# Softplus of both layers by a cubic in two factors, and dt's bias as a row of a matrix product

## The chip, the cores and the metric

The kernel runs on one core of one Trainium2 chip. The metric is the device time of one execution in microseconds. A core has TensorE (PE: matrix products, into the eight banks of PSUM), VectorE (DVE), ScalarE (ACT), GpSimd (POOL) and SyncE (SP, which issues most of the DMAs). Each engine runs its own instructions in program order and waits at semaphores for the others.

## The reference

One image of 64 x 64 pixels with 96 channels goes through two layers. Each layer is a token mixer (a selective scan over the 4096 pixels, in several directions) and then an MLP 96 -> 384 -> 96 in an emulated 8-bit float. Both mixers compute, from the convolved and activated u (192 channels), a step length dt for every pixel and channel, and dt is what the change is about:

```python
x_dbl = u @ x_proj_w
dt = x_dbl[..., :DT_RANK]                                # 6 columns
B_mat, C_mat = ...                                       # 16 columns each
dt = jax.nn.softplus(dt @ dt_proj_w + dt_proj_b)
```

Then layer 0 forms `decay = exp(cumsum(dt * A))` and sums of `dt * B * u` weighted by it. Layer 1 runs the recurrence `h = exp(dt * A) * h + dt * u * B; y = sum(h * C)`, over 192 channels x 16 states, along rows and columns, forwards and backwards. For x of either sign, softplus(x) = max(x, 0) + log(1 + exp(-|x|)).

## The kernel before, in words

**The softplus.** ScalarE forms |t + bias| and from it z = sigmoid(-|t + bias| - ln 2); log(1 + exp(-|x|)) is z times a polynomial of degree four in z squared (`LOG1P`). VectorE forms the positive part and adds.

**Layer 0** (to about 104 us of the profile). `norm_in0` normalises the image and projects it. The decays of layer 0 fall to nothing so fast that only the first 160 steps at either end of each direction count (`scan_ends`): `x_proj(d)` makes the rows of four directions (L732, L733, copied by ScalarE at L734), `dt_proj(j)` makes t for three units of 128 x 320 (L739, L743) and gives ScalarE four operations each (L749 Abs, L750 Relu, L751 Sigmoid, L752 Square), and `log1p(j)` calls `polynomial` (L993, three times L995, L996, L997: six VectorE operations). The products of `x_proj` and `dt_proj` share a pool of two PSUM banks, which are taken in turn: four x_proj and three dt_proj in the order xe0, xe1, de0, xe2, xe3, de1, de2. The main convolution's taps (`conv0`, L644 and L645, its SiLU at L634) are put between by `others(n)`. All of it is kept in program order on every engine; on VectorE the casts of both MLPs' weights (L2496, L2500), which wait for their DMAs, come ahead of `scan_ends`. After `log1p` VectorE goes on with L792, the running sums of dt (L795) and their products (L807); ScalarE then loads a table and takes L816 and L828.

**The middle** (about 104 to 303 us). `middle` collects the rest of layer 0 and the beginning of layer 1 in an `Order`: every operation is added with its engine, an estimated cost in us, what it reads and writes and which buffers it takes. `Order.run` is a list scheduler. It plays the plan through with these costs, one operation at a time; among the operations that can start earliest it takes the one with the highest rank, which is the longest path to the end by the costs, plus the group's `LEAD`. The result is the program order of each engine. So costs and leads decide the order, and nothing else in the program. The groups are `mix0` (layer 0's gating and output, four pairs of chunks of 512 pixels), `compose1` (layer 1's convolution weights), `mlp0` (L1497 up, L1524 down, L1540 back, L1471 to L1477 `norm`, L1528 the bias), `conv_unit` (layer 1's convolution: products L1584 and L1586, combined by VectorE at L1611 to L1616, sigmoid L1619, u at L1620) and `project`. The projections wait for the last image rows (POOL, L1551), the sigmoids of `conv_unit` for the last square root of a norm.

`project(c, m, last)` runs four times: for (0,0), (0,1), (4,0) and (4,1), each on two chunks of 128 channels and half of the narrow 64. It makes x_dbl's rows (L1650, L1653) in two banks; ScalarE copies them to the buffer xd (L1656); `step_products` (L1695) and `step_products_n` (L1699) make t for three units of 128 x 512, in three banks. The weights lie twice in `w_dt1`, at partitions 0 to 5 and 96 to 101 (`RANKS`), filled by two DMAs (L1287) in `open1`. `softplus(i)` is the unit's work:

```python
o.add("ACT", 0.68, lambda: keep(act(vz(), at[t], AF.Abs, bias=bias)), ...)                 # L1714
o.add("DVE", 0.73, lambda: keep(dve.tensor_scalar(d(), at[t], bias, 0.0, ALU.add, ALU.max)), ...)   # L1715
o.add("ACT", 0.7, ... AF.Sigmoid ...)                                                      # L1716
o.add("ACT", 0.6, ... AF.Square ...)                                                       # L1717
o.add("DVE", 0.42, lambda: keep(dve.tensor_scalar(p(), vzz(), QC, QD, ALU.mult, ALU.add)), ...)     # L1718
```

and after that two more Squares on ScalarE (L1719, L1720) and three VectorE operations (L1721, L1722, L1723). `d` lies in the unit's dt buffer, `p` in its du buffer. Then dt times u is formed in the du buffer (L1727, L1730; POOL, in the last project VectorE), dt is copied by columns (L1736), and both are stored (L1767 to L1778). For the narrow units there is one dt and one du buffer (`ye`), for the wide ones two.

The last project also starts layer 1's scans: `spread4` products (L1807) repeat 32 rows of du and dt over 128 partitions, ScalarE copies them (L1821), VectorE multiplies (L1811) and makes the first two row scans (L1835).

**The scans** (L2014, from 302.7 us): 24 passes of 16 scans of 128 x 1024 on VectorE, with the decays on ScalarE (L1987), products and sums on POOL (L1966, L2019, L2042) and TensorE. Their order is written out by hand (`scans`). B's rows for the first passes are loaded on SP's queue behind the stores of the last project. At the end comes the last MLP.

Of the kernel before, what the change touches and what calls it, by code (L numbers as in the profile page):

```python
# [39 lines left out]
P = 128  # L40
# [21 lines left out]
RANKS = (slice(0, RANK), slice(96, 96 + RANK))  # L62
# [15 lines left out]
QA = LOG1P[3] / (4 * LOG1P[4])  # L78
QB = (LOG1P[2] / LOG1P[4] - 6 * QA**2) / 2
QC = LOG1P[1] - LOG1P[4] * (4 * QA**3 + 4 * QA * QB)  # L80
QD = LOG1P[0] - LOG1P[4] * (QA**2 + QB) ** 2

# [44 lines left out]
CARRIED = (0, 1, 2, 5, 7)  # L127
IN_DVE, OTHERS = (), (15, 9, 9)
# [10 lines left out]
LEAD = {"compose": -84.0}  # L139
LEAD |= {("mix", s): t for s, t in enumerate((1589.0, 1847.0, -1582.0, -1562.0))}  # L140
LEAD |= {("mlp", s): t for s, t in enumerate((1510.0, 80.0, 777.0, -2488.0))}
LEAD |= {("conv", 0, 0): 702.0, ("conv", 0, "n"): 2071.0, ("conv", 0, 1): -2872.0}
LEAD |= {("conv", 4, 0): -611.0, ("conv", 4, "n"): 13.0, ("conv", 4, 1): -2041.0}
LEAD |= {("project", 0, 0): -579.0, ("project", 0, 1): -3064.0, ("project", 4, 0): 470.0, ("project", 4, 1): -3512.0}
# [120 lines left out]
class Net:  # L265
    def __init__(self, ctx, tc, x, out):
# [23 lines left out]
        self.qa = self.column("qa", QA)  # L290
        self.qb = self.column("qb", QB)
# [399 lines left out]
    def scan_ends(self, ep, pm, ps, pad, ue, beside):  # L691
# [44 lines left out]
        def dt_proj(j):  # L736
# [13 lines left out]
            keep(nc.scalar.activation(dt[:, s, :], t, AF.Relu, bias=bias))  # L750
            keep(nc.scalar.activation(z[:, s, :], z[:, s, :], AF.Sigmoid, bias=self.nln2, scale=-1.0))  # L751
            keep(nc.scalar.activation(zz[:, s, :], z[:, s, :], AF.Square))  # L752

        def log1p(j):
            s = slice(2 * j, 2 * j + 2)
            self.polynomial(z[:, s, :], zz[:, s, :], dt[:, s, :], p[:, s, :], keep)
# [233 lines left out]
    def polynomial(self, z, zz, dt, p, keep):  # L990
# [6 lines left out]
        keep(nc.vector.tensor_tensor(dt, dt, p, ALU.add))  # L997

# [251 lines left out]
    def open1(self, w, kp, rp):  # L1250
# [35 lines left out]
        for r in RANKS:  # L1286
            nc.sync.dma_start(self.w_dt1[r], w["w_dt"])  # L1287
# [68 lines left out]
    def mix0(self, s):  # L1356
# [30 lines left out]
        for c in chunks:  # L1387
            o.add("PE", 0.95, mean(c), r=[("y0", c)], new={("m", c): "bank"})
        o.add("PE", 1.1, mean_n, r=both, w=[("m", c) for c in chunks])
        for c, r in zip(chunks, LANES):  # L1390
            o.add("DVE", 0.67, centre(c), r=[("m", c)], w=[("y0", c)])
            o.add("DVE", 0.67, centre_n(c, r), r=[("m", c)], w=[("y1", c)])
# [10 lines left out]
        for i, (key, y, r) in enumerate(squares):  # L1403
            o.add("PE", 0.95, variance(i, key), r=[key], **({"w": [("v", s)]} if i else {"new": {("v", s): "bank"}}))
# [1189 lines left out]
```

## Time and profile before

| what | value |
|---|---|
| median of 3 runs | 1218.54 us (1215.86 to 1219.69) |
| the profiled execution | 1217.9 us, span 1216.1 us |
| busy share of the span | PE 84%, DVE 93%, ACT 74%, POOL 69% |
| mean granted TensorE clock | 0.872 of full speed |
| first scan of L2014 starts | 302.72 us |
| last product of layer 1's convolution ends | 262.86 us |
| DMA | 183.10 MB, mean 151 GB/s |

A span is the time from the first to the last instruction of the profiled execution. In a list of groups each line has the source line, engine, operation, output <- inputs with their shapes and the count; then busy us, mean ns of one; then the engine's idle time before them and what ended it. In a timeline a line begins with the start and the duration in us, and the bracket tells the idle time before. PEclk is the share of TensorE's clock that was granted.

### The profile page before, as it was taken

What the parts mean: (1) busy time and instruction counts of PE and PEld (TensorE: products, weight loads), DVE (VectorE), ACT (ScalarE), POOL (GpSimd) and SP (SyncE); (2) the same over time, 40 slices, a digit from 0 to 9 for tenths busy, and PEclk for the clock granted to TensorE, in tenths of its full rate; (3) what the DMA queues carried; (4) which work ended last, traced back from release to release, by engine and by line L of the source; (5) the groups of instructions that cost most, each with busy time, mean ns of one, the idle gap of its engine ahead of it and who ended that gap; (6) DMA issues with size and microseconds to landing.
All of it is one profiled execution on the core that took longest, in us unless ns stands there. A gap on an engine that the chain in (4) does not pass through costs nothing.

```text
span 1216.1 us, 11204 instructions
## 1 busy us (share of the span) xinstructions
PE 1017.9 (84%) x3488; PEld 414.6 (34%) x3488; DVE 1129.2 (93%) x908; ACT 905.4 (74%) x1177; POOL 841.6 (69%) x510
## 2 busy tenths in 40 slices
PE   9998889985278877888888877898778898899886
PEld 5533333321023322222332322233224443344344
DVE  7895887688898999999999999999999999999978
ACT  5683654656578888887888878888888888898626
POOL 3002464352678888888798788988898887887756
PEclk9998999985589788798878788888789999888987
DMA  2262011376764583575734685545747767343301
GB/s 77 64 180 52 7 21 32 116 254 187 238 192 132 171 250 128 174 229 175 240 99 137 203 251 181 180 131 176 240 129 208 221 194 265 97 143 93 104 1 52
DMA packets 79128, 183.10 MB, mean 151 GB/s; under 512 B 21534, under 2 KB 34936, under 8 KB 77688
## 3 DMA queue, kind: packets, MB, share of 16 engines
q1 hardware_dynamic: 78376, 182.16, 48.2%
q8 instruction: 28, 0.46, 0.2%
q10 hardware_dynamic: 688, 0.19, 0.1%
q14 instruction: 36, 0.29, 0.1%
HBM read 159.73 MB, written 21.52 MB: 149 GB/s over the span
## 4 chain that ended last, share of the span: by engine, by line
DVE 37%; PE 19%; issue 8%; ACT 7%; DMA 3%; POOL 1%; SPq 0%; DVEq 0%; POOLq 0%; ACTq 0%
DVE xws L2014 12%; PE hs L2025 10%; DVE h1s L2014 10%; DVE h0s L2014 8%; PE hs L2029 4%; ACT da L1987 3%; DVE x2s L2014 3%; ACT xws L1972 2%; DVE x1s L2014 2%; DVE x0s L2014 2%; DMA kept<-xn 2%; DMA x2s<-bc 1%; PE acc L2053 1%; PE da L2343 1%; POOL hss L2019 1%
## 5 line engine op out<-in xcount | busy, mean ns | idle before, releaser
L2042 POOL TENSOR_TENSOR kept<-kept,kept 128x1024 f32<-128x1024 f32 x92 | 217.1, 2359 | 83.8 <-issue 45.0
L2019 POOL TENSOR_TENSOR hss<-h1s,xws 128x1024 f32<-128x1024 f32 x96 | 228.0, 2377 | 48.7 <-DVE xws L2014 47.1
L2025 PE MATMUL hs<-h0s,ident 128*128 128x512 f32 x360 | 224.8, 711 | 29.2 <-DVE h0s L2014 24.6
L1987 ACT ACTIVATE da<-dt1s,a 128x1024 f32<-128x1024 f32 x168 | 187.4, 1116 | 58.0 <-DVE xws L2014 49.0
L2014 DVE TENSOR_TENSOR_SCAN xws<-da,xws 128x1024 f32<-128x1024 f32 x96 | 221.5, 2307 | 7.3 <-ACT da L1987 7.2
L1987 ACT ACTIVATE da<-dt0s,a 128x1024 f32<-128x1024 f32 x166 | 185.2, 1115 | 27.2 <-DVE h0s L2014 10.0
L2029 PE MATMUL hs<-hss,ident 128*128 128x512 f32 x368 | 187.8, 602 | 8.1 <-POOL hss L2019 7.9
L2014 DVE TENSOR_TENSOR_SCAN h1s<-da,xws 128x1024 f32<-128x1024 f32 x69 | 156.0, 2261 | 0.0
L2053 PE MATMUL acc<-kept,fold 128*32 128x512 f32 x368 | 87.0, 683 | 71.8 <-POOL kept L2042 71.8
L2038 ACT COPY kept<-hs 128x512 f32<-128x512 f32 x184 | 107.7, 585 | 43.7 <-PE hs L2029 43.5
L2025 PEld LDWEIGHTS hs<-h0s,ident 128*128 128x128 f32 x360 | 72.4, 219 | 155.2 <-issue 82.4
L2029 PEld LDWEIGHTS hs<-hss,ident 128*128 128x128 f32 x368 | 70.3, 194 | 107.8 <-issue 79.4
L2025 PE MATMUL hs<-x1s,ident 128*128 128x512 f32 x128 | 75.7, 676 | 12.6 <-DVE x1s L2014 12.6
L2025 PE MATMUL hs<-x0s,ident 128*128 128x512 f32 x128 | 74.2, 664 | 13.5 <-DVE x0s L2014 13.5
L2025 PE MATMUL hs<-x2s,ident 128*128 128x512 f32 x120 | 72.9, 693 | 12.1 <-DVE x2s L2014 12.1
L1966 POOL TENSOR_TENSOR x1s<-x1s,dus 128x1024 f32<-128x1024 f32 x32 | 75.6, 2366 | 8.8 <-DMA x1s<-bc 8.8
L1966 POOL TENSOR_TENSOR x2s<-x2s,dus 128x1024 f32<-128x1024 f32 x32 | 75.7, 2366 | 1.3 <-DMA x2s<-bc 1.2
L2014 DVE TENSOR_TENSOR_SCAN x0s<-da,x0s 128x1024 f32<-128x1024 f32 x32 | 73.5, 2296 | 1.3 <-ACT da L1987 1.2
L2014 DVE TENSOR_TENSOR_SCAN x1s<-da,x1s 128x1024 f32<-128x1024 f32 x32 | 73.4, 2293 | 1.3 <-ACT da L1987 1.3
L2014 DVE TENSOR_TENSOR_SCAN x2s<-da,x2s 128x1024 f32<-128x1024 f32 x32 | 73.5, 2298 | 1.0 <-ACT da L1987 0.9
L1972 ACT COPY xws<-x1s 128x1024 f32<-128x1024 f32 x32 | 63.0, 1970 | 5.2 <-POOL hss L2019 5.2
L1966 POOL TENSOR_TENSOR x0s<-x0s,dus 128x1024 f32<-128x1024 f32 x28 | 66.3, 2367 | 0.0
(379 smaller groups left out, 1913.3 us busy)
## 6 DMA issues: line engine op xcount, KB each, us to landing
kept<-bc SPq DMA_DIRECT2D x92, 512.0 KB
x2s<-bc SPq DMA_DIRECT2D x32, 512.0 KB
x0s<-bc SPq DMA_DIRECT2D x28, 512.0 KB
x1s<-bc SPq DMA_DIRECT2D x28, 512.0 KB
dus<-du SPq DMA_DIRECT2D x20, 512.0 KB
dt1s<-dt SPq DMA_DIRECT2D x20, 512.0 KB
dt0s<-dt SPq DMA_DIRECT2D x20, 512.0 KB
kept<-xn SPq DMA_DIRECT2D x24, 384.0 KB
```

What stands on the lines that cost most here:

```text
L1966: keep(nc.gpsimd.tensor_tensor(x, x, du[:, part[j]], ALU.mult))
L1972: keep(copy(grid(xw)[:, w, :], cols(xs[i % 3])[:, w, :]))
L1987: keep(nc.scalar.activation(t, dts[o][:, part[j]], AF.Exp, scale=self.a6[:, g, k : k + 1]))
L2014: keep(nc.vector.tensor_tensor_scan(to, da, x, start, ALU.mult, ALU.add))
L2019: keep(nc.gpsimd.tensor_tensor(cols(hs)[:, w, :], grid(h1)[:, w, :], grid(xw)[:, w, :], ALU.add))
L2025: keep(nc.tensor.matmul(t, self.ident, x[:, chunk(m)], start=k == 0, stop=False))
L2029: keep(nc.tensor.matmul(sums[i, m], self.ident, hs[:, chunk(m)], start=False, stop=True))
L2038: keep(nc.scalar.copy(to, sums.pop((i, j * (SC // CH) + h))))
L2042: keep(nc.gpsimd.tensor_tensor(t, t, times_c_by(i, a), ALU.mult))
L2053: keep(nc.tensor.matmul(to, self.fold4, src, start=k == 0, stop=k == NK - 1))
L2343: keep(nc.tensor.matmul(o[:, j], y[r, 2 * k + j : CH : 4], w[r], start=first and j == 0, stop=end and j == 1))
```

## The change

In both layers log(1 + exp(-|x|)) becomes z times a cubic in z squared, written in two factors: z (zz + b)((s zz + a)^2 + c), with zz = z squared. The second factor's square is a ScalarE Square with a scale and a bias column; what remains are three VectorE operations.

- Layer 1, `softplus(i)`: ScalarE has Abs (without a bias), Sigmoid, Square, and a Square that writes into the du buffer. VectorE has three operations of three operands; the last takes the positive part of t from its PSUM bank and adds. L1715, L1718 and one Square are gone.
- dt's bias is a seventh row of `w_dt1`, filled by two more DMAs (a column of `vec` as one row of 256 numbers). The matching row of ones in xd comes from the copies of L1656, which become an Identity with the column `unit` as its bias; `unit` is made at the start by POOL.
- Layer 0: Relu moves from ScalarE to VectorE, emitted in `dt_proj`, ahead of all three `log1p`; the second factor's Square takes its place on ScalarE; `polynomial`'s six operations become two in `cubic` and an add.
- The middle's planner gets other costs for many operations and other leads. `norm` and `biased` get switches (`NORM0_ACT`, `BIAS0_POOL`) which are empty.

```diff
-RANKS = (slice(0, RANK), slice(96, 96 + RANK))
+RANKS = (slice(0, RANK + 1), slice(96, 96 + RANK + 1))
...
+CUBIC = (0.34226051, 1.83304455, -0.33816952, 3.07350780)
+QS = math.sqrt(CUBIC[0])
+QB = CUBIC[0] * CUBIC[3]
...
-LEAD = {"compose": -84.0}
-LEAD |= {("mix", s): t for s, t in enumerate((1589.0, 1847.0, -1582.0, -1562.0))}
-LEAD |= {("mlp", s): t for s, t in enumerate((1510.0, 80.0, 777.0, -2488.0))}
-LEAD |= {("conv", 0, 0): 702.0, ("conv", 0, "n"): 2071.0, ("conv", 0, 1): -2872.0}
-LEAD |= {("conv", 4, 0): -611.0, ("conv", 4, "n"): 13.0, ("conv", 4, 1): -2041.0}
-LEAD |= {("project", 0, 0): -579.0, ("project", 0, 1): -3064.0, ("project", 4, 0): 470.0, ("project", 4, 1): -3512.0}
+LEAD = {"compose": -466.0}
+LEAD |= {("mix", s): t for s, t in enumerate((1515.0, 1828.0, -2023.0, -2022.0))}
+LEAD |= {("mlp", s): t for s, t in enumerate((1271.0, 97.0, 799.0, -3939.0))}
+LEAD |= {("conv", 0, 0): 780.0, ("conv", 0, "n"): 2081.0, ("conv", 0, 1): -2885.0}
+LEAD |= {("conv", 4, 0): -1313.0, ("conv", 4, "n"): 535.0, ("conv", 4, 1): -1773.0}
+LEAD |= {("project", 0, 0): -1484.0, ("project", 0, 1): -3461.0, ("project", 4, 0): -289.0, ("project", 4, 1): -3808.0}
...
-        self.qa = self.column("qa", QA)
-        self.qb = self.column("qb", QB)
+        self.qa = self.column("qa", QS * CUBIC[2])
+        self.unit = self.column("unit", 0.0)
+        for r in RANKS:
+            nc.gpsimd.tensor_tensor(self.unit, self.unit, self.ident[:, r.stop - 1 : r.stop], ALU.add)
...
             keep(nc.scalar.activation(z[:, s, :], t, AF.Abs, bias=bias))
-            keep(nc.scalar.activation(dt[:, s, :], t, AF.Relu, bias=bias))
+            keep(nc.vector.tensor_scalar(dt[:, s, :], t, bias, 0.0, ALU.add, ALU.max))
             keep(nc.scalar.activation(z[:, s, :], z[:, s, :], AF.Sigmoid, bias=self.nln2, scale=-1.0))
             keep(nc.scalar.activation(zz[:, s, :], z[:, s, :], AF.Square))
+            keep(nc.scalar.activation(p[:, s, :], zz[:, s, :], AF.Square, bias=self.qa, scale=QS))
...
-            self.polynomial(z[:, s, :], zz[:, s, :], dt[:, s, :], p[:, s, :], keep)
+            self.cubic(z[:, s, :], zz[:, s, :], p[:, s, :], keep)
+            keep(nc.vector.tensor_tensor(dt[:, s, :], dt[:, s, :], p[:, s, :], ALU.add))
...
+    def cubic(self, z, zz, p, keep):
+
+        nc = self.nc
+        keep(nc.vector.scalar_tensor_tensor(p, p, QB, z, ALU.add, ALU.mult))
+        keep(nc.vector.scalar_tensor_tensor(p, zz, CUBIC[1], p, ALU.add, ALU.mult))
...
-            nc.sync.dma_start(self.w_dt1[r], w["w_dt"])
+            nc.sync.dma_start(self.w_dt1[r.start : r.start + RANK], w["w_dt"])
+            nc.sync.dma_start(self.w_dt1[r.stop - 1 : r.stop], w["vec"][:, 1:2].rearrange("d o -> o d"))
...
-            o.add("PE", 0.95, mean(c), r=[("y0", c)], new={("m", c): "bank"})
+            o.add("PE", 0.88, mean(c), r=[("y0", c)], new={("m", c): "bank"})
...
-        o.add("DVE", 0.4, biased, r=["narrow"], w=[("o16", c)])
-        o.add("DVE", 0.7, lambda: keep(nc.vector.tensor_tensor(x, x, at["o16", c], ALU.add)), r=[("o16", c)], w=[("res", c)])
+        o.add(*(("DVE", 0.78), ("POOL", 1.2))[c in BIAS0_POOL], biased, r=["narrow"], w=[("o16", c)])
+        o.add("DVE", 0.69, lambda: keep(nc.vector.tensor_tensor(x, x, at["o16", c], ALU.add)), r=[("o16", c)], w=[("res", c)])
...
-        o.add("DVE", 1.22, lambda: keep(nc.vector.tensor_tensor(u(), u(), at["sg", name], ALU.mult)), r=[("sg", name)], w=[("u", name)])
+        o.add("DVE", 1.5, lambda: keep(nc.vector.tensor_tensor(u(), u(), at["sg", name], ALU.mult)), r=[("sg", name)], w=[("u", name)])
...
-            return lambda: keep(nc.scalar.copy(at[xd][:, k], at["x", n, k][0:XE]))
+            return lambda: keep(nc.scalar.activation(at[xd][:, k], at["x", n, k][0:XE], AF.Identity, bias=self.unit[0:XE]))
...
-            o.add("ACT", 0.68, lambda: keep(act(vz(), at[t], AF.Abs, bias=bias)), r=[t], new={w: "w1" if g and not last else "w"}, w=[z])
-            o.add("DVE", 0.73, lambda: keep(dve.tensor_scalar(d(), at[t], bias, 0.0, ALU.add, ALU.max)), r=[t, hold], w=[kd])
+            o.add("ACT", 0.6, lambda: keep(act(vz(), at[t], AF.Abs)), r=[t], new={w: "w1" if g and not last else "w"}, w=[z])
             o.add("ACT", 0.7, lambda: keep(act(vz(), vz(), AF.Sigmoid, bias=self.nln2, scale=-1.0)), r=[w], w=[z], table="sigmoid")
             o.add("ACT", 0.6, lambda: keep(act(vzz(), vz(), AF.Square)), r=[z, w], w=[zz])
-            o.add("DVE", 0.42, lambda: keep(dve.tensor_scalar(p(), vzz(), QC, QD, ALU.mult, ALU.add)), r=[zz, w, hold_u], w=[ku])
-            o.add("ACT", 0.7, lambda: keep(act(vzz(), vzz(), AF.Square, bias=self.qa)), r=[w], w=[zz])
-            o.add("ACT", 0.7, lambda: keep(act(vzz(), vzz(), AF.Square, bias=self.qb)), r=[w], w=[zz])
-            o.add("DVE", 0.69, lambda: keep(dve.scalar_tensor_tensor(p(), vzz(), LOG1P[4], p(), ALU.mult, ALU.add)), r=[zz, w, hold_u], w=[ku])
-            o.add("DVE", 0.69, lambda: keep(dve.tensor_tensor(p(), p(), vz(), ALU.mult)), r=[z, w, hold_u], w=[ku])
-            o.add("DVE", 0.69, lambda: keep(dve.tensor_tensor(d(), d(), p(), ALU.add)), r=[ku, hold, hold_u], w=[kd])
+            o.add("ACT", 0.7, lambda: keep(act(p(), vzz(), AF.Square, bias=self.qa, scale=QS)), r=[zz, w, hold_u], w=[ku])
+            o.add("DVE", 0.63, lambda: keep(dve.scalar_tensor_tensor(p(), p(), QB, vz(), ALU.add, ALU.mult)), r=[z, w, hold_u], w=[ku])
+            o.add("DVE", 0.63, lambda: keep(dve.scalar_tensor_tensor(p(), vzz(), CUBIC[1], p(), ALU.add, ALU.mult)), r=[zz, w, hold_u], w=[ku])
+            o.add("DVE", 0.63, lambda: keep(dve.scalar_tensor_tensor(d(), at[t], 0.0, p(), ALU.max, ALU.add)), r=[t, ku, hold, hold_u], w=[kd])
...
-            o.add("DVE", 0.69, times_b(i, lambda i=i: self.du[:, chunk(i)]), r=[("DU", (0, i % 2))], w=[("xs0", i)])
+            o.add("DVE", 1.1, times_b(i, lambda i=i: self.du[:, chunk(i)]), r=[("DU", (0, i % 2))], w=[("xs0", i)])
```

The other cost changes are of the same kind: a 512-column product from 0.95 or 0.98 to 0.88 or 0.9, a VectorE operation on 128 x 512 from 0.69 to 0.63, L1524's products from 1.1 to 0.8, L1506 from 0.58 to 0.45.

## The prediction

> **What bounds the kernel now.** I read the page's chain and its costliest groups first.
>
> ```profile
> DVE 37%; PE 19%; issue 8%; ACT 7%; DMA 3%; POOL 1%; SPq 0%; DVEq 0%; POOLq 0%; ACTq 0%
> ...
> L2014 DVE TENSOR_TENSOR_SCAN xws<-da,xws 128x1024 f32<-128x1024 f32 x96 | 221.5, 2307 | 7.3 <-ACT da L1987 7.2
> ```
>
> The layer 1 scans on VectorE (L2014) own the long end of the program. The change touches none of them; it can only move the moment when the first one starts. So next the busy times by stretch (columns: PE, PEld, DVE, ACT, POOL busy us, granted clock, DMA share, GB/s).
>
> ```profile
> 145.00:206.00 61.00, 54.17 (x254) 21.85 (x255) 49.58 (x110) 30.66 (x62) 33.86 (x46) 0.94 0.10 20
> 206.00:255.00 49.00, 47.48 (x141) 16.20 (x140) 34.49 (x49) 30.60 (x47) 22.18 (x19) 0.97 0.42 126
> 255.00:300.00 45.00, 31.84 (x56) 10.36 (x54) 39.55 (x55) 27.83 (x45) 13.35 (x10) 0.62 0.74 245
> 300.00:1163.00 863.00, 709.83 (x1866) 276.36 (x1866) 851.64 (x388) 704.90 (x828) 712.06 (x330) 0.86 0.56 176
> ```
>
> From 300 on VectorE is busy 851.64 of 863 us, so a microsecond won before 300 arrives at the end nearly whole. From 206 to 255 TensorE is the bound (idle 1.5 us); VectorE has 14 us to spare there. Only from 263, where the last convolution product ends, do VectorE and ScalarE set the pace. Of layer 0's softplus I read the timeline by engine (start, duration, engine, line):
>
> ```profile
> 47.00 0.52 ACT L750 ACTIVATE dte<-de,vec 128x320 f32<-128x320 f32 x1
> ...
> 48.12 0.50 PE L732 MATMUL xe<-ue,wx 128*80 128x160 f32 x2
> ...
> 49.81 0.21 DVE L2500 CAST b<-b2q 128x96 f32<-128x96 fp8e5 x1
> ...
> 65.08 0.69 ACT L634 ACTIVATE y<-c,vec 128x512 f32<-128x512 f32 x1 [5.85 <-PE c L645]
> ...
> 67.28 1.28 ACT L816 ACT_TABLE_LOAD   x1 [0.32 <-DVE v L807]
> ```
>
> At 67.28 ScalarE's next table waits 0.32 us for VectorE; TensorE had released ScalarE only just before (L634 ends at 66.96). Two chains meet there almost level. And of layer 1's end:
>
> ```profile
> 263.71 1.30 DVE L1721 SCALAR_TENSOR_TENSOR xws<-h1s,xws 128x512 f32<-128x512 f32 x2
> ...
> 267.33 2.28 DVE L1620 TENSOR_TENSOR kept<-kept,kept 128x1024 f32<-128x1024 f32 x1
> ...
> 270.59 3.74 PE L1653 MATMUL bank<-kept,kept 128*102 128x512 f32 x4
> ...
> 284.14 1.30 DVE L1721 SCALAR_TENSOR_TENSOR kept<-h1s,kept 128x512 f32<-128x512 f32 x2 [1.68 <-ACT h1s L1720]
> ...
> 288.50 3.78 PE L1807 MATMUL bank<-kept,kept 32*128 32x512 f32 x4 [8.57 <-DVE kept L1727]
> 292.08 7.03 PE L1807 MATMUL bank<-hss,kept 32*128 32x512 f32 x8
> ...
> 302.72 2.28 DVE L2014 TENSOR_TENSOR_SCAN h1s<-da,xws 128x1024 f32<-128x1024 f32 x1
> ...
> 318.54 4.64 POOL L1966 TENSOR_TENSOR x1s<-x1s,dus 128x1024 f32<-128x1024 f32 x2 [8.82 <-DMA x1s<-bc]
> ```
>
> Read it as one chain: the last product ends (262.86), the last u is formed (267.33), projected (270.59), softplus begins (278.07), ends (287.77), is spread over partitions by TensorE (to 299.1), and the first scan starts (302.72).
>
> **The sum is made against the profiled execution:** 1217.9 us, span 1216.1. The median shown is 1218.54, 0.6 more; I don't correct for it. A measurement of this kernel tells some 0.3%, 3.7 us, from no change.
>
> **Layer 1's units, the work.** The prices by shape:
>
> ```profile
> L1715 DVE TENSOR_SCALAR xws<-bank,kept 128x512 f32<-128x512 f32 x6 | 4.2, 746 | 3.9 <-ACT h1s L1714 3.9
> L1718 DVE TENSOR_SCALAR xws<-h1s 128x512 f32<-128x512 f32 x6 | 3.6, 629 | 0.3 <-ACT h1s L1717 0.2
> L1722 DVE TENSOR_TENSOR xws<-xws,h1s 128x512 f32<-128x512 f32 x6 | 3.9, 682 | 0.0
> ```
>
> There are 12 units. Each loses L1715 (0.75) and L1718 (0.41 undisturbed, 0.63 mean) and keeps three VectorE operations of 0.68, now all of three operands (L1721 costs the same 0.69). VectorE loses 12 x 1.2 = 14 us; ScalarE loses one Square, 12 x 0.62 back to back = 7 us. Of the eight copies L1656 (0.59) each takes a bias and becomes like L1714 (0.67): 0.7 us in all, 0.2 on the last chain. A matmul over 7 rows for 6 has as many columns: nothing. Until 263 all of this lies beside TensorE's products and is worth nothing; were that cover gone, at most the 11.0 us that TensorE idles from 104 to 263 could be won.
>
> **Layer 1's end.** (a) 262.86 to 278.07: ScalarE starts the last sigmoid 0.6 late, at 264.19, behind L1720 of the project before; u waits from 265.14 to 267.33 behind that project's six Horner operations, two of which go; L1653 waits 1.0 for a spread (268.59 to 270.59) in front of it on TensorE. Of these 3.8 us I take 2.5, since six VectorE operations of 0.61 remain around. (b) 278.07 to 287.77: two units, ScalarE eight operations instead of ten; the last Square ends at about 282.9 instead of 284.7, six VectorE operations of 0.61 follow the first unit's Square at 282.2 and end at 285.9: 1.9 won. (c) 287.77 to 302.72 is 14.95 us in which VectorE idles 0.75. L1715 and L1718 of the narrow unit (1.1) go, and its other three can fill those idles: 13.1 us. TensorE's way is no shorter than that: six spreads (10.6), copy and exponential (1.7), du0's product: 13.1 as well. So 1.8. Sum 6.2, less 0.2 for the copies: 6.0 won. Bounds: 2, if (a) and (c) are taken by the spread and the transfers; 10, if all 3.8 of (a) come and L1653 and L1695 run at full clock (half of 3.74 and of 2).
>
> Here a rule can be weighed. From 268.6 to 278 TensorE is busy without a gap, and the rows grant 0.50 throughout, after an idle of 3.7 us. The Trainium skill's page "TensorE: Matmul & The Clock Gate", section "Part 1: The HAM clock gate", has the gate open after about 3.4 us of sustained work. By it the last step products and perhaps the spreads would run at full rate; this trace disagrees, so my sum keeps the half rate.
>
> **New waits in layer 1.** The second Square writes into the du buffer, so ScalarE, not VectorE, waits until POOL and the store have left it, with the next unit's Abs and the sigmoids queued behind. The one narrow buffer is the tight case: its store is issued by 262.5, and ScalarE needed it at 271; nothing. The bank of t is now read by the unit's last operation, some 6 us later than by L1715, and the products queue behind it when the eight banks run out. In 206 to 255 TensorE waited 1.5 us in all: taken at nothing, bound 3.
>
> **Layer 0's units.** In each of three units VectorE's six operations (0.32, 3 x 0.51, 2 x 0.49: 2.8 us) become four (a relu of some 0.5, 3 x 0.5: 2.0). Relu moves from ScalarE to VectorE and a Square takes its place: ScalarE is even. But VectorE's order puts the first relu behind the weight casts, which wait for their DMA and end at 50.0. The bank that it reads is the one that the fourth x_proj (L732 at 48.12) writes next: there are two, taken in turn. Before, L750 had left it at 47.5. Now L732 starts at 50.5, after a relu of some 0.5 (L1715 scaled to 320 columns), 2.4 late. The 0.44 that TensorE waited for L734 is absorbed; the convolution taps behind are late by 1.9. They release L634, whose end moves from 66.96 to 68.8, and the table load from 67.28 to 68.8: 1.5 lost, though VectorE itself is 0.6 early. From there exponentials and scans follow one another with no slack (VectorE is busy 41.35 of 44 us from 60 to 104). Bounds: 0.3 won (the wait at 67.28, if the bank is free in time), 2.5 lost (the whole delay).
>
> **Set-up.** Two DMAs more, each of 256 single numbers, on SP's queue behind L1287 and L1290, which end at 114.0; SP then waits until 116.87 for ScalarE. An L1290 costs 0.42 to issue; at twice that each they end at 115.8. Their rows are needed at 218. Nothing, bound 0.6 if packets delay the small transfer of 116.87. Two small POOL additions stand before 1 us of waits for DMA: nothing.
>
> **The order.** New costs and leads rearrange the work from 104 to 263. The work is the same; TensorE is idle 11.0 us there, 6.5 of it in two waits for normalised rows (L1477) near 146 and 157. Bounds: 6 won, if these go; 13 lost, if there are two more pairs. I take 0, the present idle.
>
> **The first scans.** POOL idles 8.82 us until 318.54 for x1's second half, which is issued after the narrow unit's copies (POOL to 303.75), and VectorE then waits 2.69 at 328.55. The narrow unit ends earlier relative to the scans: 1 won; bounds 3.3 won, 2 lost (the DMA share is 1.02 from 310 to 320).
>
> **Sum:** +1.5 - 6.0 + 0 - 1.0 = -5.5: 1212.4.
>
> **Rivals.** *Hidden anyway:* spreads and transfers hold the first scan, the tail gives 3, the first scans 0: -1.5, 1216.4. For it: TensorE's way in (c) is as long as VectorE's. Against: its beginning moves with (a) and (b). *More:* the waits at 146 and 157 go or the clock stays up: 6 more, 1206. For it: the new costs take bias and gating operations as long as the trace has them under contention. *Slower:* the last MLP pair, whose lead falls from -2488 to -3939, leaves TensorE waiting for normalised rows before the projections can open (POOL's last image now ends at 214.15). One such pair of waits is 6.5; it decides for slower from 9.2 us on, and two pairs give 1212.4 + 13 = 1225. Against: only 0.5 us of idle stand in 190 to 206 now. *Doesn't do what it says:* layer 0 shortens VectorE's work and lengthens the stage; that is in the sum, not a case.
>
> **Chances.** Forecast 0.50 (own range 1208 to 1215.5, from the tail's 2 to 10 with the rest), hidden 0.22, more 0.14, slower 0.14. A little of the forecast lies within 0.3%: faster 0.60, same 0.26, slower 0.14. The range 1205 to 1220.5 leaves out nearly all of slower and the far end of more.
>
> **What would show it.** Right: the fourth x_proj (L732 at 48.12) starts after 50; L816's load near 68.8; first L2014 at 297 to 299; Abs to last add of the last wide units near 8 us; no wait of 2.69 near 325. Wrong: TensorE idle of over 11 us before the last product, or the first scan not earlier than 301.

## The result, and the profile after

| | before | after |
|---|---|---|
| median of 20 runs each | 1216.77 us | 1214.91 us |
| ratio after / before, 95% interval | | 0.9988 [0.9973, 1.0003] |
| profiled execution, its span | 1217.9, 1216.1 us | 1215.23, 1213.3 us |

The change is worth 0.1%, and the interval still touches 1: no difference that this measurement can tell. The forecast was 1212.4 us, faster by 0.45%. The time lies in the range given (1205 to 1220.5), but it is made of larger pieces of both signs than the sum on record. I cut both spans at the same three moments: the first mean product of the middle, the end of the last convolution product, the first scan.

| stretch | before | after | difference | forecast |
|---|---|---|---|---|
| start to first mean product (layer 0) | 102.50 | 109.19 | +6.7 | +1.5 |
| to the end of the last convolution product (the order) | 160.4 | 157.6 | -2.8 | 0 |
| to the first scan (layer 1's end) | 39.9 | 33.7 | -6.2 | -6.0 |
| to the end (the scans) | 913.4 | 912.8 | -0.6 | -1.0 |

The page after, the chain and the group of scans on VectorE: still the same bound.

```profile
DVE 37%; PE 17%; ACT 9%; issue 9%; DMA 3%; POOL 2%; DVEq 0%; SPq 0%; POOLq 0%; ACTq 0%
...
L2033 DVE TENSOR_TENSOR_SCAN xws<-da,xws 128x1024 f32<-128x1024 f32 x96 | 222.4, 2317 | 8.2 <-ACT da L2006 8.1
```

Busy times by stretch, after (columns: PE, PEld, DVE, ACT, POOL busy us, granted clock, DMA share, GB/s):

```profile
52.00:62.00 10.00, 10.00 (x46) 2.60 (x42) 4.76 (x10) 5.48 (x10) 0.00 (x0) 0.51 0.50 149
...
145.00:206.00 61.00, 51.98 (x262) 21.20 (x262) 56.38 (x116) 32.53 (x67) 41.84 (x53) 0.97 0.10 20
206.00:255.00 49.00, 49.00 (x154) 17.62 (x150) 31.91 (x42) 26.65 (x41) 23.09 (x21) 1.00 0.37 113
255.00:300.00 45.00, 31.71 (x63) 10.44 (x62) 35.84 (x42) 26.32 (x41) 15.49 (x11) 0.70 0.82 263
300.00:1163.00 863.00, 706.51 (x1866) 275.66 (x1866) 851.08 (x388) 703.35 (x827) 710.32 (x330) 0.87 0.56 176
```

The same ten microseconds before the change:

```profile
52.00:62.00 10.00, 10.00 (x96) 3.64 (x100) 9.13 (x20) 6.12 (x11) 0.00 (x0) 1.00 0.66 183
```

From 52 to 62 TensorE is busy throughout in both, but the recorded products are 46 for 96, at a granted clock of 0.51 for 1.00. From 206 to 255 TensorE is busy 49.00 of 49 us; the banks of t that are held longer cost nothing there. The timeline after, layer 0 (start, duration, engine, line; in brackets the idle time before it and its releaser):

```profile
50.12 0.54 DVE L752 TENSOR_SCALAR dte<-de,vec 128x320 f32<-128x320 f32 x1
...
50.72 0.50 PE L734 MATMUL xe<-ue,wx 128*80 128x160 f32 x2 [2.30 <-DVE dte L752]
...
53.49 1.43 PE L741 MATMUL de<-xe,w_dt 6*128 6x320 f32 x2
...
73.97 1.28 ACT L820 ACT_TABLE_LOAD   x1
```

The mechanism is the one that was forecast: the relu on VectorE (L752) starts at 50.12, and the fourth x_proj waits for its bank until 50.72 (forecast 50.5). But the table load behind it is 6.7 late (67.28 to 73.97), not 1.5. And layer 1's end:

```profile
262.24 4.56 PE L1609 MATMUL bank<-pairs,cw 96*128 96x512 f32 x10
...
277.84 1.14 PE L1718 MATMUL bank<-h1s,kept 7*128 7x512 f32 x4
278.90 1.07 PE L1722 MATMUL bank<-h1s,kept 7*64 7x512 f32 x4
279.01 1.09 ACT L1736 ACTIVATE h1s<-bank 128x512 f32<-128x512 f32 x2 [1.22 <-PE bank L1718]
...
286.86 3.78 PE L1826 MATMUL bank<-kept,kept 32*128 32x512 f32 x4 [6.89 <-DVE kept L1746]
...
290.44 7.03 PE L1826 MATMUL bank<-hss,kept 32*128 32x512 f32 x8
...
300.47 2.27 DVE L2033 TENSOR_TENSOR_SCAN h1s<-da,xws 128x1024 f32<-128x1024 f32 x1
...
316.56 4.65 POOL L1985 TENSOR_TENSOR x1s<-x1s,dus 128x1024 f32<-128x1024 f32 x2 [9.10 <-DMA x1s<-bc]
```

From the end of the last product (266.8) it is 12.2 us to Abs, 8.4 to the end of dt (287.4), 13.05 to the first scan. L1722, the narrow unit's four step products, stands on TensorE's queue ahead of the spreads L1826, the first of which wait 6.89 for dt times u (L1746). That place becomes important below.

### The profile page after: what moved, and what is told of

It reads as the page before. It is cut to its first block, busy times and chain, and to the rows that moved or that the text cites. A ratio compares the mean times of both kernels' runs of the same rounds, so it can differ in the third digit from the quotient of the medians.

```text
span 1213.3 us, 11155 instructions
## 1 busy us (share of the span) xinstructions
PE 1011.2 (83%) x3488; PEld 413.4 (34%) x3488; DVE 1118.5 (92%) x878; ACT 898.1 (74%) x1165; POOL 843.3 (70%) x512
## 4 chain that ended last, share of the span: by engine, by line
DVE 37%; PE 17%; ACT 9%; issue 9%; DMA 3%; POOL 2%; DVEq 0%; SPq 0%; POOLq 0%; ACTq 0%
DVE xws L2033 12%; DVE h1s L2033 9%; PE hs L2044 8%; DVE h0s L2033 7%; PE hs L2048 4%; ACT da L2006 4%; ACT xws L1991 3%; DVE x0s L2033 3%; DVE x2s L2033 2%; DVE x1s L2033 2%; DMA dt<-hss 1%; PE acc L2072 1%; DMA kept<-xn 1%; POOL hss L2038 1%; PE da L2362 1%
## 5 line engine op out<-in xcount | busy, mean ns | idle before, releaser
L2061 POOL TENSOR_TENSOR kept<-kept,kept 128x1024 f32<-128x1024 f32 x92 | 216.8, 2357 | 83.1 <-issue 39.8
L2038 POOL TENSOR_TENSOR hss<-h1s,xws 128x1024 f32<-128x1024 f32 x96 | 228.2, 2379 | 49.2 <-DVE xws L2033 47.8
L2048 PE MATMUL hs<-hss,ident 128*128 128x512 f32 x368 | 191.3, 612 | 14.8 <-POOL hss L2038 14.5
L2044 PE MATMUL hs<-x2s,ident 128*128 128x512 f32 x120 | 67.9, 649 | 12.9 <-DVE x2s L2033 12.9
```

The source lines that it names most:

```text
L2038: keep(nc.gpsimd.tensor_tensor(cols(hs)[:, w, :], grid(h1)[:, w, :], grid(xw)[:, w, :], ALU.add))
L2044: keep(nc.tensor.matmul(t, self.ident, x[:, chunk(m)], start=k == 0, stop=False))
L2048: keep(nc.tensor.matmul(sums[i, m], self.ident, hs[:, chunk(m)], start=False, stop=True))
L2061: keep(nc.gpsimd.tensor_tensor(t, t, times_c_by(i, a), ALU.mult))
```

## The experiments

Each ratio is to the kernel before, from runs of both on the same chip. Single executions scatter by several us (after: 1209.5 to 1223.6), and after the first scan the profiled executions alone differ by 8 us (909.2 to 917.4). So what a part is worth is read from its stretch of the trace; the ratio tells whether it arrives.

### Layer 0 taken out, and alone

Theory: layer 0's relu costs more than its 1.5 us, and the gain is all layer 1's. Rival: both parts are near zero.

The changed kernel with layer 0's units as before (`e1_l0_as_before`):

```diff
-            keep(nc.vector.tensor_scalar(dt[:, s, :], t, bias, 0.0, ALU.add, ALU.max))
+            keep(nc.scalar.activation(dt[:, s, :], t, AF.Relu, bias=bias))
...
-            keep(nc.scalar.activation(p[:, s, :], zz[:, s, :], AF.Square, bias=self.qa, scale=QS))
...
-            self.cubic(z[:, s, :], zz[:, s, :], p[:, s, :], keep)
-            keep(nc.vector.tensor_tensor(dt[:, s, :], dt[:, s, :], p[:, s, :], ALU.add))
+            self.polynomial(z[:, s, :], zz[:, s, :], dt[:, s, :], p[:, s, :], keep)
```

> The changed kernel with layer 0's three units as before (Relu on ScalarE, the polynomial of six VectorE operations); layer 1's units, the bias row, costs and leads stay changed. Theory 1 (the relu behind the weight casts holds a PSUM bank, TensorE stands still 2.3 us and its clock is halved for 10 us): the first mean product (L1377 in the changed kernel) starts at 102.5 instead of 109.2, the first scan at 293.8 instead of 300.5, the time is 6.7 us below the changed kernel: ratio to the kernel before 0.993 to 0.994. Rival (what layer 0 loses is paid back later, since the middle waits for DMA or its order anyway): the time is that of the changed kernel, ratio 0.9985.

Measured: 1209.1 us, ratio 0.993 [0.9906, 0.9953].

The kernel before with the same hunk the other way round (`e2_l0_alone`):

> The kernel before with layer 0's part of the change alone (relu on VectorE, Square with a scale on ScalarE, cubic of two VectorE operations and an add). Theory 1: TensorE idles 2.3 us at 48.4, the granted clock is 0.50 from 52 to 61, the first mean product starts at 109.2 instead of 102.5, the time is 6.7 us above the kernel before: ratio 1.0055. Rival (the middle absorbs it): ratio 1.000 to 1.001. Second rival (fewer VectorE operations win in layer 0, as the number of instructions says): ratio 0.998.

Measured: 1221.24 us, ratio 1.0035 [1.0017, 1.0052]; first mean product at 109.17, with a pause of 2.33 us before the fourth x_proj.

So the halves are +0.35% and -0.7%, and cancel in part: they add to -0.35%, and both together measured -0.12% (-0.27 to +0.03). Layer 0's part is a loss by itself.

### The pause, and what it does to the clock

Theory: what makes 1.9 us of delay into 6.7 is the halved clock behind the pause. Filling the pause with convolution taps, which otherwise come later, takes it away; nothing else is changed. `e3_taps3` fills all of it, `e4_tap1` one microsecond of it (`others(1)` and 14):

```diff
-IN_DVE, OTHERS = (), (15, 9, 9)
+IN_DVE, OTHERS = (), (12, 9, 9)
...
         x_proj(2)
+        others(3)
         x_proj(3)
```

> The changed kernel with three of the 15 later convolution taps moved between the third and the fourth x_proj, so that TensorE has work while the bank is held; the number of operations and the moment at which the bank comes free stay. Theory 1 (it is TensorE's idle time and the clock that follows it): no idle, granted clock 1.00 throughout, the first mean product near 103, the time 6 us below the changed kernel: ratio 0.994. Rival (it is the later relu and the later dt on VectorE and ScalarE, not TensorE): the fourth x_proj starts at 51 as it does now and dt is ready no sooner, so at most 1 us is won: ratio 0.998.

> The same with a single tap moved: TensorE's idle time is 1.4 us instead of 2.3. If the halved clock follows any pause of over 1 us: clock 0.50 from 52 on, 1 us won against the changed kernel, ratio 0.998. If a pause of 1.4 us is too short for it: clock 1.00, 5 to 6 us won, ratio 0.994 to 0.995.

Measured: `e3_taps3` 1213.27 us, ratio 0.9968 [0.9942, 0.9994]; no pause, first mean product at 104.61, and the clock at 1.00 from 52 to 62:

```profile
52.00:62.00 10.00, 10.00 (x84) 3.40 (x87) 5.53 (x12) 7.68 (x13) 0.00 (x0) 1.00 0.44 124
```

`e4_tap1` 1213.85 us, ratio 0.9973 [0.9952, 0.9994]; first mean product at 103.45. Its TensorE in the timeline:

```profile
50.21 0.50 PE L734 MATMUL xe<-ue,wx 128*80 128x160 f32 x2 [1.30 <-DVE dte L752]
```

and its busy times by stretch (columns as above):

```profile
50.00:62.00 12.00, 11.79 (x98) 4.22 (x102) 6.88 (x14) 7.72 (x14) 0.00 (x0) 1.00 0.45 131
```

The pause is only 1.0 us shorter than in the changed kernel, and the first mean product comes 5.7 us earlier: the clock stayed up. That is the missing term of the front. (It stayed up in this execution; the last section shows why another one may differ.) Both kernels still hold the bank for the relu, and both are 0.3% faster than the kernel before, the intervals ending just under 1; `e1_l0_as_before` is better still. But the ratios missed what was expected, 0.994 to 0.995: against the changed kernel's 0.9988 they show some 2 us, known to 3 or 4, of the 4.6 and 5.7 us that the front won in the profiles. Where the rest went is open.

### The relu's place, and the cubic

Is it the relu's place or the cubic? The changed kernel with only the relu back on ScalarE (`e8_relu_scalar`):

```diff
-            keep(nc.vector.tensor_scalar(dt[:, s, :], t, bias, 0.0, ALU.add, ALU.max))
+            keep(nc.scalar.activation(dt[:, s, :], t, AF.Relu, bias=bias))
```

> The changed kernel with layer 0's relu back on ScalarE in its place after Abs, the cubic kept (ScalarE has one operation more per unit, VectorE three). Theory: what cost the front was only where the relu stands (behind the weight casts on VectorE, holding the bank), not the cubic: no idle time over 0.6 us in front of the fourth x_proj, a clock near 1.00 from 52 to 62, first mean product at 102 to 104.5, ratio 0.992 to 0.994. Rival (the cubic's second Square on ScalarE delays ScalarE's next table as well): first mean product at 105 or later, ratio 0.995 or more.

Measured: 1210.27 us, ratio 0.995 [0.9932, 0.9969]; first mean product at 106.68. The wait for VectorE is gone, but there is a new one: ScalarE's list is one Square longer, the copy of x_dbl (L736) comes later, and TensorE waits for it. The timeline:

```profile
51.66 0.86 PE L741 MATMUL de<-xe,w_dt 6*128 6x320 f32 x2 [1.04 <-ACT xe L736]
```

and the stretches behind it:

```profile
52.50:59.00 6.50, 6.50 (x33) 1.89 (x36) 3.07 (x7) 6.02 (x11) 0.00 (x0) 0.50 0.40 111
59.00:59.50 0.50, 0.50 (x12) 0.21 (x8) 0.40 (x2) 0.00 (x0) 0.00 (x0) 0.90 0.84 256
59.50:62.00 2.50, 2.50 (x28) 0.79 (x24) 2.50 (x6) 0.20 (x1) 0.00 (x0) 1.00 0.94 298
```

My theory (only the relu's place) fell: the second Square in its place costs too, again by a pause (1.04 us) with some 6.8 us of half clock behind it. Even `e1_l0_as_before`, whose pause is that of the kernel before (0.43 for 0.44), shows 3.4 us at half clock (below). So two more kernels put a tap into this pause: `e9_late_square` (`e8_relu_scalar` with the second Square moved behind all products of layer 0's projection) and `e11_l0_as_before_tap` (`e1_l0_as_before`; of the diff only the tap, its last two parts):

```diff
-            keep(nc.scalar.activation(p[:, s, :], zz[:, s, :], AF.Square, bias=self.qa, scale=QS))
         def log1p(j):
             s = slice(2 * j, 2 * j + 2)
+            keep(nc.scalar.activation(p[:, s, :], zz[:, s, :], AF.Square, bias=self.qa, scale=QS))
...
-IN_DVE, OTHERS = (), (15, 9, 9)
+IN_DVE, OTHERS = (), (14, 9, 9)
...
-        others(1)
+        others(2)
         dt_proj(1)
```

> The changed kernel with layer 0's relu on ScalarE after Abs, its second Square moved behind the last products of layer 0's step projection (just ahead of the cubic), and one convolution tap more ahead of the second step product. Theory: what is left of the front's loss without the relu on VectorE is the pause of 0.4 to 1.0 us ahead of the second step product, behind which the clock is halved for 3 to 6 us; with ScalarE's list ahead of it as in the kernel before and a tap in the pause, the clock stays at 1.00 from 52 to 62, first mean product at 101.5 to 103, ratio 0.990 to 0.993. Rival (the later Squares delay the cubic and ScalarE's next table): mean product at 104 or later, ratio 0.994 or more, with a clock of 1.00.

> The changed kernel with layer 0 as before (0.993) and one convolution tap more ahead of the second step product, where TensorE paused 0.43 us and then showed half the clock for some 3 us. Theory: the small pause also costs clock: 1.00 from 52 to 62, first mean product at 102 to 103 instead of 104.4, ratio 0.991 to 0.993. Rival (that dip was not the pause's): the clock dips again without a pause, mean product at 104 or later, ratio 0.993 to 0.995.

Measured: `e9_late_square` 1210.8 us, ratio 0.996 [0.9945, 0.9975]; clock 1.00, first mean product at 102.92 (as expected; the ratio is not, 0.990 to 0.993 was). `e11_l0_as_before_tap` 1207.0 us, ratio 0.9929 [0.9909, 0.9949]; clock 1.00, first mean product at 102.40, that is 2.0 earlier than without the tap. Its stretch:

```profile
50.00:62.00 12.00, 12.00 (x110) 4.20 (x106) 10.85 (x23) 6.77 (x12) 0.00 (x0) 1.00 0.57 158
```

The pause and the half clock behind it (0.43 and half of 3.4, together 2.1) were the 1.9 us that `e1_l0_as_before` had been late. In the ratio that step does not show (0.993 both times). And even with no pause the cubic gains layer 0 nothing: 102.92 against 102.40 with the polynomial. The plan behind it is the same in both, yet took 191.6 us to the first scan with the cubic and 189.3 without. With one profile of each that tells little: the seven kernels with this plan and nothing moved behind layer 0 took 189.3 to 192.9 us. `e11_l0_as_before_tap` beats both kernels, level with `e1_l0_as_before`: layer 1's part of the change without layer 0's.

### Operations and plan

Behind layer 0, the way from the first mean product to the first scan fell from 200.2 to 191.3 us. Is that the shorter softplus, or the planner's new costs and leads? `e5_order_as_before` is the changed kernel with the costs and leads of before (those of the softplus's own operations stay); `e6_order_alone` is the kernel before with the new ones:

```diff
-LEAD = {"compose": -466.0}
+LEAD = {"compose": -84.0}
...
-            o.add("PE", 0.88, mean(c), r=[("y0", c)], new={("m", c): "bank"})
+            o.add("PE", 0.95, mean(c), r=[("y0", c)], new={("m", c): "bank"})
...
-        o.add("PE", 1.0, step_products_n, r=ready, new={dtn: "dtn", dun: "dun", ("t", n, 2): "bank"})
+        o.add("PE", 1.1, step_products_n, r=ready, new={dtn: "dtn", dun: "dun", ("t", n, 2): "bank"})
```

> The changed kernel with the planner's costs and leads of before; the operations of both layers as changed. Theory: of the 8 us that the layer 1 part is worth without layer 0 (0.993), some 5 to 6 come from the shorter softplus behind the last convolution product and 2 to 3 from the new costs and leads in the stretch before it. Then the first mean product starts at 109 as in the changed kernel, the stretch from it to the last convolution product returns to about 160 us, and from there to the first scan it stays near 34 us; ratio to before about 1.001. Rival (the new costs and leads carry the tail too, by placing the last project's units better): that distance goes back to 38 to 40 us, ratio about 1.005. Rival (costs and leads are worth nothing, the 2.8 us were a longer wait by chance): the stretch stays at 157.6, ratio 0.999.

> The kernel before with only the new costs and leads; every operation of both softpluses as before. Theory: the first mean product stays at 102.5, the stretch from it to the last convolution product falls from 160.4 to about 158 us, from there to the first scan stays near 40 us; ratio to before 0.997 to 0.999. Rival (leads chosen for the short units misfit the long ones): the stretch or the tail is longer than before, ratio above 1.002. Rival (costs and leads carry everything): 34 us behind the last product, ratio 0.993.

Measured: `e5_order_as_before` 1221.09 us, ratio 1.0035 [1.0019, 1.0051]. `e6_order_alone` 1229.45 us, ratio 1.0105 [1.0076, 1.0134]. I had the two as terms that add. They don't. Two more runs divide the plan: `e10_leads_as_before` is the changed kernel with only the leads of before, `e12_three_costs` is `e5_order_as_before` with the three raised costs:

```diff
-        o.add(*(("DVE", 0.4), ("POOL", 1.2))[c in BIAS0_POOL], biased, r=["narrow"], w=[("o16", c)])
+        o.add(*(("DVE", 0.78), ("POOL", 1.2))[c in BIAS0_POOL], biased, r=["narrow"], w=[("o16", c)])
...
-        o.add("DVE", 1.22, lambda: keep(nc.vector.tensor_tensor(u(), u(), at["sg", name], ALU.mult)), r=[("sg", name)], w=[("u", name)])
+        o.add("DVE", 1.5, lambda: keep(nc.vector.tensor_tensor(u(), u(), at["sg", name], ALU.mult)), r=[("sg", name)], w=[("u", name)])
...
-            o.add("DVE", 0.69, times_b(i, lambda i=i: self.du[:, chunk(i)]), r=[("DU", (0, i % 2))], w=[("xs0", i)])
+            o.add("DVE", 1.1, times_b(i, lambda i=i: self.du[:, chunk(i)]), r=[("DU", (0, i % 2))], w=[("xs0", i)])
```

> The changed kernel with only the leads of before; the planner's new costs stay. With both of before the way from the first mean product to the first scan was 198.7 us, with both new it is 191.3. Theory: the leads shift the units by whole microseconds while the costs change by tenths, so the leads carry most of the 7.4: 196 to 199 us here, ratio 1.002 to 1.004. Rival (the costs, by which the planner knows the true length of the gating and bias operations): 191 to 193, ratio 0.999 to 1.000.

> The changed kernel with the planner's costs and leads of before, except the three costs that were raised: the narrow bias addition 0.78 for 0.40, the gating product 1.50 for 1.22, the product of du with B 1.10 for 0.69. With all costs of before the way from the first mean product to the first scan was 198.7 us, with all new costs and the leads of before 191.3. Theory: these three, which the planner had too short, carry most of the 7.4: 191 to 194 us, ratio 0.998 to 1.000. Rival (the many small cuts of 0.02 to 0.1 on TensorE and VectorE carry it): 196 to 199 us, ratio 1.002 to 1.004.

Measured: `e10_leads_as_before` 1213.93 us, ratio 0.9981 [0.9964, 0.9999]; `e12_three_costs` 1223.27 us, ratio 1.0055 [1.0037, 1.0074]. All of them by stretch, us (one profiled execution each; layer 0 as changed in all but the kernel before and `e6_order_alone`):

| kernel | softplus of layer 1 | plan | mean product to last product | to the first scan | together |
|---|---|---|---|---|---|
| before | before | before | 160.4 | 39.9 | 200.2 |
| `e2_l0_alone` | before | before | 160.6 | 38.0 | 198.7 |
| `e5_order_as_before` | after | before | 162.3 | 36.4 | 198.7 |
| `e12_three_costs` | after | before, three costs after | 158.8 | 39.8 | 198.7 |
| `e6_order_alone` | before | after | 159.3 | 53.3 | 212.5 |
| `e10_leads_as_before` | after | leads before, costs after | 157.7 | 33.5 | 191.3 |
| after | after | after | 157.6 | 33.7 | 191.3 |

The shorter softplus under the plan of before is worth nothing (198.7 against `e2_l0_alone`'s 198.7, ratio 1.0035 both times), the new plan under the old softplus costs 12.3 us, and both together gain 7.4 to 8.9. The leads do nothing (191.3 both times); the three raised costs move work between the two stretches and gain nothing. So, by elimination, the costs that were cut, by 0.01 to 0.3 each, are needed; no run has them alone. Seven profiles of the new plan had 155.7 to 159.2 us in the first stretch and 33.5 to 33.8 in the second, so of the totals 198.7, 212.5 and 191.3 the differences are clear of the scatter, and a difference of 2 or 3 us in one first stretch is not. How such small cuts can do it, TensorE's timeline of `e5_order_as_before` shows:

```profile
280.77 1.97 PE L1718 MATMUL bank<-h1s,kept 7*128 7x512 f32 x4
290.15 2.07 PE L1826 MATMUL bank<-kept,kept 32*128 32x512 f32 x2 [7.42 <-DVE kept L1746]
292.15 1.97 PE L1722 MATMUL bank<-h1s,kept 7*64 7x512 f32 x4
294.05 2.07 PE L1826 MATMUL bank<-kept,kept 32*128 32x512 f32 x2
```

and its ScalarE:

```profile
294.17 0.60 ACT L1736 ACTIVATE h1s<-bank 128x512 f32<-128x512 f32 x1 [7.31 <-PE bank L1722]
```

The narrow unit's step products (L1722) stand behind two spread products, which wait 7.42 for dt times u (L1746); their own inputs, the copies of x_dbl, had ended at 281.57. So ScalarE begins the narrow unit at 294.17, 12.2 us behind the first wide one (281.93); in the changed kernel it is 4.8 (279.01 to 283.77). `e12_three_costs` has the same order (L1722 at 292.27). In `e6_order_alone` they (there L1699) stand behind six spread products, the first four of which wait:

```profile
293.25 3.78 PE L1807 MATMUL bank<-kept,kept 32*128 32x512 f32 x4 [12.05 <-DVE kept L1727]
296.82 1.91 PE L1807 MATMUL bank<-hss,kept 32*128 32x512 f32 x2
298.66 1.97 PE L1699 MATMUL bank<-h1s,kept 6*64 6x512 f32 x4
```

That the changed places go with the longer distances is shown; that this one place is all of the 7.4 us is not, since other places move too.

### The first scans

The wait of 2.69 (after: 2.97) near 326 was to shrink because the narrow unit would end earlier. In the changed kernel its end moved with the first scan, since its last operations stand between and behind the row scans on VectorE. `e7_narrow_first` puts the row scans behind them:

```diff
-            o.add("DVE", 2.33, row_scan(j), r=["xs", ("da", j), *rows, *([("row", 0)] if j else [])], w=[("row", j)])
+            o.add("DVE", 2.33, row_scan(j), r=["xs", ("da", j), *rows, ("dt", n, 2), *([("row", 0)] if j else [])], w=[("row", j)])
```

> The changed kernel with the two row scans put behind the narrow unit's last three operations on VectorE (no operation more or less). Theory: the last scans' start lost its forecast microsecond because the narrow unit's end stayed 2.7 us in front of the first scan, behind the row scans; with it first, its last operation ends near 292 instead of 297.8, the copies on GpSimd near 296, the wait of 9.1 us for x1's second half falls to 3 to 5, and VectorE's wait of 2.97 near 326 goes; the first scan stays at 300.5 within 0.5; ratio to the kernel before about 0.9965. Rival (the wait near 326 is set by the transfers, not by the narrow unit): the wait stays within 1 us, ratio 0.998 to 0.999. Rival (the row scans' own successors, the second half of x2's B and the copies, become late): first scan at 302 or a new wait of 2 us, ratio 1.000.

Measured: 1215.24 us, ratio 0.9995 [0.998, 1.0011]. The timeline of VectorE, GpSimd and ScalarE:

```profile
291.44 0.69 DVE L1742 SCALAR_TENSOR_TENSOR ye<-bank,ye 128x512 f32<-128x512 f32 x1
...
316.98 4.66 POOL L1985 TENSOR_TENSOR x1s<-x1s,dus 128x1024 f32<-128x1024 f32 x2 [11.36 <-DMA x1s<-bc]
...
323.99 1.95 ACT L1991 COPY xws<-x1s 128x1024 f32<-128x1024 f32 x1 [5.33 <-POOL hss L2038]
...
327.00 2.35 DVE L2033 TENSOR_TENSOR_SCAN xws<-da,xws 128x1024 f32<-128x1024 f32 x1 [2.82 <-ACT da L2006]
```

The narrow unit ended 5.65 us earlier (from 297.78 to 292.13), GpSimd was free earlier and waited the longer (11.36 for 9.10): x1's second half started at 316.98, the wait stayed at 2.82. The rival holds: the transfer decides, not the narrow unit. VectorE's wait names ScalarE, but ScalarE had itself waited 5.33 for GpSimd's sums (L2038), which stand behind x1's second half. SP issued that transfer from 303.79 to 304.34, in the changed kernel from 304.64 to 307.02, so earlier by less than the 5.65 us, and GpSimd still got it no earlier; whether its place in the queue or the traffic holds it was not tested.

## Why the prediction was right or wrong

- **Layer 0's units, +1.5 forecast, +6.7 measured.** Order, bank, pause and the delay of the fourth x_proj came as forecast; the sum's term was mis-sized. It took the pause as 1.9 us of delay, part of it absorbed, and left out the clock. From 51.6 to 61.8 it was 0.50 (half-microsecond rows below): 10.2 us at half rate are 5.1 us of TensorE's work, and 1.9 + 5.1 = 7.0 against 6.7. The upper bound of 2.5, "the whole delay", was none. `e3_taps3`, without a pause, had the clock at 1.00 and 4.6 us of the 6.7 back.
- **The order, 0 forecast, -2.8 measured**, and the more important fault: I took operations and plan as separate steps. By the table above neither alone gains anything. That the total still lies in the range is in part luck: by the stretches layer 0 cost 5.2 us more than forecast, and 2.8 of that came back here.
- **Layer 1's end, -6.0 forecast, -6.2 measured**: (a) -3.0 for -2.5, (b) -1.3 for -1.9, (c) -1.9 for -1.8. The working holds for a plan in which the narrow unit's step products stay ahead of the spreads, as in the kernel before. That the new plan would keep them there was not argued, and with the costs of before it does not: there the end took 36.4 to 39.8 us, not 33.7. The sum was right on a condition that I had not seen.
- **The clock in the tail.** I kept the half rate. Measured: half from 270.0 to 276.8, full to 280.2, then half again. The step products L1718 ran in the full stretch (1.14 us for four, before 2.02 for three of them).
- **What would show it.** Abs to the last add took 8.4 us (near 8 forecast); the first scan at 300.47 missed 297 to 299, by what layer 0 lost beyond the forecast less what the order won.
- **The work**: 14 us of VectorE and 7 of ScalarE were to go in layer 1, and 2.4 of VectorE in layer 0. Over the program VectorE is 10.7 less busy (1129.2 to 1118.5), not 16.4, and ScalarE 7.3. Of the 5.7 that are missing 4.4 lie in the first three narrow units, where L1740 and L1741 took 1.58 and 1.28 us on average and L1721 and L1722, before, 0.71 and 0.69; why is open.
- **Longer-held banks of t: nothing**, right: TensorE did not idle from 206 to 255.
- **The first scans, -1.0 forecast, -0.6 measured** over the whole rest, and the wait did not shrink at all. The cause named (the narrow unit's copies) was wrong; `e7_narrow_first` showed the transfer.
- **The rivals.** The *slower* one hung on the last MLP pair's lead, and the leads move nothing (`e10_leads_as_before`). TensorE's waits for normalised rows did not go, as *more* would have it (6.7 before, 5.8 after). *Hidden anyway*, nearest in time with 1216.4, is wrong in its mechanism: the tail gave all its 6 us, and layer 0 took them.

## What to carry to other kernels

An operation that changes engine takes a place in the new engine's list: look at what stands ahead of it there, which buffer it holds meanwhile, and price a pause of TensorE by the clock behind it as well as by its length. Where a planner with a table of costs lays out the work, operations and costs are one change: measure them together, and look in each queue for work that is ready but stands behind work that waits. A change that moves a time by nothing may still hold a gain and a loss; taking its parts out one at a time found a version 0.7% faster than the kernel before.

## What the runs showed of the hardware

The halved clock lasted whole multiples of about 3.4 us. The granted clock is read here in short rows, and the moment of a switch from the share of a row; `e1_l0_as_before`, behind a pause of 0.43 us:

```profile
51.50:52.00 0.50, 0.50 (x4) 0.19 (x4) 0.47 (x2) 0.10 (x1) 0.00 (x0) 1.00 0.00 0
52.00:52.50 0.50, 0.50 (x4) 0.00 (x0) 0.47 (x2) 0.50 (x2) 0.00 (x0) 0.78 0.02 5
52.50:55.50 3.00, 3.00 (x18) 1.04 (x20) 2.47 (x6) 2.94 (x7) 0.00 (x0) 0.50 0.05 9
55.50:56.00 0.50, 0.50 (x8) 0.10 (x4) 0.47 (x2) 0.48 (x2) 0.00 (x0) 0.80 0.26 59
```

A row of 0.78 is half clock for 0.22 us of its 0.5, so the clock was halved from 52.28 to 55.70, 3.4 us. `e8_relu_scalar` (pause 1.04) had it from 52.27 to 59.1, 6.8 us. The changed kernel (pause 2.30):

```profile
51.50:52.00 0.50, 0.50 (x6) 0.31 (x8) 0.00 (x0) 0.32 (x1) 0.00 (x0) 0.56 0.00 0
52.00:61.50 9.50, 9.50 (x42) 2.54 (x38) 4.27 (x9) 5.48 (x10) 0.00 (x0) 0.50 0.48 138
61.50:62.00 0.50, 0.50 (x9) 0.06 (x8) 0.49 (x1) 0.00 (x0) 0.00 (x0) 0.70 0.92 345
```

51.56 to 61.80: 10.2 us, three times 3.4, though TensorE was busy throughout. In the tail of the same kernel it was half for 6.8 us and full for 3.4.

The moments fit too. In each of the fourteen traces all switches up to 330 us lie whole multiples of 3.413 us apart, to 0.02 us. In the changed kernel they are at 51.56, 61.80, 106.17, 113.00, 167.61, 171.02, 270.01, 276.84, 280.25 and 328.04: 3, 13, 2, 16, 1, 29, 2, 1 and 14 steps.

The Trainium skill's page "TensorE: Matmul & The Clock Gate", section "Part 1: The HAM clock gate", has an activity window of about 3.4 us that runs freely, not from the start of the work. The steps agree with that. For the clock to open, its table asks for one busy window or more: here it took one, two or three.

The length of the pause does not decide alone: 1.30 us (`e4_tap1`) and 0.44 us (before) left the clock up, 0.43 us (`e1_l0_as_before`) halved it for 3.4 us. Part of that may be where the pause falls in the steps, counted back or on from a switch. In the changed kernel it lies whole in one of them (48.42 to 50.72, in 48.15 to 51.56), and the clock fell at the end of that step. In `e4_tap1` a boundary at 49.83 splits the pause (48.91 to 50.21) into 0.92 and 0.38. The boundaries lie differently from trace to trace (the clock fell at 51.56 in the changed kernel, at 50.45 in `e7_narrow_first`), so a pause of 1.30 is not shown to be safe in every execution. It is not all of it: in the kernel before and in `e1_l0_as_before` the pause lies whole in one step, and only the second lost the clock. What else counts stays open, as does why the second and third window stayed at half.
